# Turning softmax exponentials by VectorE blocks and DMAs instead of TensorE in a two-layer cross-attention kernel

## The chip, the cores and the metric

The kernel runs on one core of a Trainium2 chip, in float32. The metric is the device time of one execution in microseconds, as the median of several runs. The profile is one execution taken by the hardware profiler. Engines are named as the profile names them: PE is TensorE's matrix multiply and PEld its weight load, DVE is VectorE, ACT is ScalarE, POOL is GpSimd, SP is the engine that issues most DMAs. "L400" is line 400 of the kernel.

## The reference, cut to what matters

Two cross-attention layers follow one another over 8 batches of 256 rows with 320 channels; the context has 256 tokens of 512 channels. There are 20 heads of 16 channels in each layer.

```python
# layer 0: 77 text tokens and 179 image tokens, two separate softmaxes
q, k, v = heads(x @ Wq.T), heads(text @ Wk.T), heads(text @ Wv.T)
k_ip, v_ip = heads(ip @ Wk_ip.T), heads(ip @ Wv_ip.T)
a = softmax(q k^T / 4) v + softmax(q k_ip^T / 4) v_ip
x1 = merge(a) @ Wo.T + bo + x

# layer 1: 252 text tokens, 4 image tokens
q, k, v = heads(x1 @ W_q), heads(text @ W_k), heads(text @ W_v)
p = softmax(q k^T / 4);  text_out = p v
qsem = l2norm(p @ text);  sem = qsem @ l2norm(ip).T
p_ip = softmax(q k_ip^T / 4 + 0.5 * sem) * mask
out = merge(text_out + p_ip v_ip) @ W_out + b_out + x1
```

The norm of `qsem` is computed without forming it: with e the exponentials, the squared norm is the sum over tokens of (e G) * e, where G = text text^T.

## The kernel before, in words

**Tiling.** A unit of work is one batch and four heads (`QUADS`), so a batch has five units (NQ = 5) and each layer 40. For each head the scores of all 256 queries against 256 keys are put in one bank of PSUM (`sc`, two halves of 128 queries). VectorE takes the negative maxima (`l0_max`, L503; `l1_max`, L716), and ScalarE writes the exponentials to SBUF with queries on the partitions (`l0_exp`, L515; `l1_exp`, L731). The next product sums over the keys, so keys have to be on the partitions: `transposed_probs` (L400) has TensorE turn each head's exponentials in four 128-column pieces back into the head's own score bank, and one copy (L407) takes them to SBUF as `et`. That copy is VectorE's for three heads of four and ScalarE's for the other.

**The value products.** `l0_values` (L533) multiplies the values v0 with `et` for four heads at once. `l1_values` (L755, L758) takes, for each half of a head, `et` as weights and streams `gv`, which holds values, normalized image tokens and G side by side. VectorE then multiplies the G part by e and sums it (L762, a reduction with a read of its accumulator) and copies the 20 value columns (L766). The results `y` have two buffers in PSUM.

**The order of the work.** It is written out by hand. The loop over n from 0 to 45 runs layer 0's unit n and, from n = 6 on, layer 1's unit n - 6. `both_layers` (n < 40) writes out one period: layer 0's scores, maxima and exponentials, its transposes between the halves of the value products of the layer-1 unit before, then layer 1's scores, maxima, exponentials and transposes, and last `l0_values`. `layer_1` does n = 40 to 45. `fillers(n, place)` is a table that puts projections, output products and the other small work of four different batches into places 0 to 7 of a period. Each compute engine runs its instructions in the order in which they are written. `masked_q` (L352, POOL) makes the masked queries that the next scores take; `l1_image` has SP copy vipA into 80 rows by four DMAs (`vip_rows`, L662), and POOL masks them.

**Loads.** SP issues, in order: inputs of the batches ahead (`xT`, `encT`, `texts`, L128, L134, L437), the residual rows `x` (L141, POOL adds the bias), `vip_rows`, and the outputs (L896). `load_late` brings the weights that layer 1 and the output products take, `ip_sb` among them, after n = 0.

Of the kernel before, what the change touches and what calls it, by code (L numbers as in the profile page):

```python
# [43 lines left out]
W1 = WV + TC1  # L44
W2 = WV + TXT1
# [5 lines left out]
def kernel(  # L51
# [85 lines left out]
    def load_resid(b):  # L137

        r = bat[b]
        r["x"] = io.tile([P, NH, C], F32, tag="x", name=f"x_{b}", bufs=1)  # L140
        nc.sync.dma_start(out=r["x"], in_=x[b].rearrange("(n p) c -> p n c", p=P))  # L141
        for half in range(NH):
            nc.gpsimd.tensor_tensor(r["x"][:, half, :], r["x"][:, half, :], bo_b, ALU.add)
# [227 lines left out]
    def unit(layer, b, g, sc, home):  # L371

# [3 lines left out]

        def pairs(pool, shape, tag, bufs):
            return [
                pool.tile(list(shape), F32, tag=tag, name=f"{tag}_{name}_{x}", bufs=bufs)
                for x in range(2)  # L380
            ]

# [4 lines left out]
            "nmx": pairs(small, nmx, f"nmx{layer}", 4),  # L387
            "e": pairs(work, (P, 2, NH, T), f"e{home}", 2 + home),
            "et": pairs(work, (P, 2, 2, NH, P), f"et{home}", 2),
        }  # L390

    def transposed_probs(u, j, tn, t0, copy=None):


        x, i = divmod(j, 2)
        ps = u["sc"][j][:tn].rearrange("p n t -> p (n t)")
        v = ps.rearrange("p (c n s) -> p c n s", c=2, n=NH)
        for c in range(2):
            for half in range(NH):
                nc.tensor.transpose(  # L400
                    v[:, c, half, :],
                    u["e"][x][:, i, half, t0 + c * tn : t0 + (c + 1) * tn],
                    ident,
                )

        copy = copy or (nc.vector.tensor_copy if j < 3 else nc.scalar.copy)
        copy(u["et"][x][:tn, i].rearrange("p c n s -> p (c n s)"), ps)  # L407
# [8 lines left out]
    v0 = [const.tile([P, 2, H, 2, D], F32, tag=f"v0_{i}", name=f"v0_{i}") for i in range(2)]  # L416
    for t in v0:
        nc.gpsimd.memset(t[:, 1, :, 0, :], 0.0)
# [3 lines left out]
    W_K1 = T + TC1 + NIP  # L422
    k1 = const.tile([P, 2, W_K1], F32, tag="k1", name="k1")

    k1c = [const.tile([P, W_K1], F32, tag=f"k1c_{i}", name=f"k1c_{i}") for i in range(2)]

# [16 lines left out]
    def l0_k(b, m):  # L443
# [24 lines left out]
        else:  # L468
# [5 lines left out]
            for rows in (low, high):  # L474
                nc.scalar.copy(kc[rows, NIP + first : T], ps[high, t0 + first : t0 + TXT1])
                if kept:
                    nc.scalar.copy(kc[rows, NIP : NIP + TXT0], kt[high, m, :])
# [45 lines left out]
    def l0_transposed(u, j, copy=None):  # L523
        transposed_probs(u, j, P, 0, copy)
# [777 lines left out]
```

## Time and profile before

| what | value |
|---|---|
| median of 3 runs | 879.38 us (879.34 to 879.57) |
| span of the profiled execution | 877.6 us |
| what lies around the span | 1.8 us, median less span |
| TensorE matmul | 863.8 us busy, 98% |
| VectorE / ScalarE / GpSimd | 612.4 / 545.0 / 208.5 us busy |
| transposes of exponentials on TensorE (L400) | 1280, 182.4 us busy |
| their copies to SBUF (L407) | 229 on VectorE, 154.4 us; 91 on ScalarE, 52.2 us |
| granted TensorE clock | 1.000 |
| DMA | 22.96 MB in 24,624 packets |
| SBUF-to-SBUF DMAs | 32, of 25 KB each (`vip_rows`) |

A row of the profile's table of groups gives line, engine, operation, what is written and read, the shapes and the count; after the bar stand the busy time in us and the mean duration in ns of one; after the second bar the engine's idle time just before them, and what ended most of it. Durations of neighbours on one engine can overlap by some hundredths of a microsecond. In a timeline the two leading numbers are start and duration in us. A line of the chain in order of time names the work that nothing else hides. A row of a table by stretches has the stretch, its length, the busy time of PE, PEld, DVE, ACT and POOL with counts, the granted clock, the share of the 16 DMA engines and GB/s.

### The profile page before, as it was taken

The page shows a single profiled execution, that of the slowest core. Times are in us where ns is not written, and L with a number is a line of the kernel's source. Part 1 is how long each engine was busy: PE and PEld are TensorE (multiplying, and loading weights), DVE is VectorE, ACT ScalarE, POOL GpSimd, SP SyncE. Part 2 cuts the span into 40 slices and gives each one's busy share as a digit, 9 for nine tenths or more (in the row PEclk, how much of TensorE's full clock was granted, in tenths as well). Part 3 has the DMA queues.
Part 4 walks back from the last instruction along what each step waited for, and adds up shares of the span by engine and source line. Part 5 has one row for each costly group of instructions (what it writes and reads, how often), then busy time and mean ns, then how long its engine had stood idle before and what let it go on. Part 6 is the DMA issues. An engine that isn't in the chain of part 4 may idle for free.

```text
span 877.6 us, 18756 instructions
## 1 busy us (share of the span) xinstructions
PE 863.8 (98%) x6184; PEld 696.3 (79%) x6184; DVE 612.4 (70%) x2071; ACT 545.0 (62%) x2386; POOL 208.5 (24%) x376
## 2 busy tenths in 40 slices
PE   8999999999999999999999999999999999999998
PEld 6777678788787887888877888888888788777876
DVE  2544477767776777876778678776777778875765
ACT  4774676556664686555765468654675558754855
POOL 2212311223211222122321322212222122312111
PEclk9999999999999999999999999999999999999999
DMA  9600100001000100001001010000100100000000
GB/s 279 174 6 16 44 1 1 2 18 41 15 2 20 34 25 2 15 22 43 17 1 21 16 43 1 3 20 16 43 1 1 22 16 1 1 21 1 1 20 16
DMA packets 24624, 22.96 MB, mean 26 GB/s; under 512 B 5936, under 2 KB 24496, under 8 KB 24528
## 3 DMA queue, kind: packets, MB, share of 16 engines
q1 hardware_dynamic: 23088, 20.27, 8.8%
q10 hardware_dynamic: 1440, 1.49, 0.5%
q8 instruction: 50, 0.82, 0.4%
q14 instruction: 46, 0.38, 0.1%
HBM read 18.31 MB, written 2.62 MB: 24 GB/s over the span
## 4 chain that ended last, share of the span: by engine, by line
PE 95%; ACT 3%; DVE 1%; DMA 1%; issue 0%; SPq 0%; POOL 0%; ACTq 0%; DVEq 0%
PE y L755 17%; PE sc L400 16%; PE v L325 11%; PE sc L362 10%; PE y L758 9%; PE k L313 8%; PE q L295 7%; PE p_o L338 6%; PE oT L533 5%; PE g L624 2%; ACT e L515 1%; PE p_aT_ps L331 1%; ACT e L731 1%; PE o L553 1%; PE ipo L877 1%; DMA wk<-in_WkT_dram 1%
## 5 line engine op out<-in xcount | busy, mean ns | idle before, releaser
L515 ACT ACTIVATE e<-sc,nmx 128x77 f32<-128x77 f32 (+1 forms) x640 | 227.2, 412 | 57.4 <-DVE nmx L503 57.4
L731 ACT ACTIVATE e<-sc,nmx 128x252 f32<-128x252 f32 x320 | 147.4, 484 | 120.0 <-DVE aip L711 107.3
L755 PE MATMUL y<-gv,et 126*128 126x272 f32 x640 | 202.0, 397 | 1.3
L762 DVE CUSTOM_DVE_ANT_0 e<-y,e 128x252 f32<-128x252 f32 x320 | 133.9, 419 | 90.4 <-PE y L758 81.8
L400 PE MATMUL sc<-ident,e 128*126 128x128 f32 (+1 forms) x1280 | 182.4, 274 | 4.2 <-ACT e L731 2.8
L407 DVE COPY et<-sc 128x512 f32<-128x512 f32 (+1 forms) x229 | 154.4, 689 | 24.3 <-PE sc L400 14.5
L503 DVE TENSOR_REDUCE nmx<-sc 128x2 f32<-128x154 f32 x320 | 109.7, 416 | 87.2 <-PE sc L362 87.2
L400 PEld LDWEIGHTS sc<-ident,e 128*126 128x126 f32 (+1 forms) x1280 | 149.1, 140 | 14.2 <-ACT e L731 6.2
L515 ACT ACTIVATION_READ_ACCUMULATOR e<-sc,nmx 128x1 f32 x640 | 159.9, 250 | 0.0
L758 PEld LDWEIGHTS y<-gv,et 126*128 126x128 f32 x640 | 120.7, 189 | 25.9
L758 PE MATMUL y<-gv,et 126*128 126x146 f32 x640 | 131.4, 287 | 0.0
L716 DVE TENSOR_REDUCE nmx<-sc 128x2 f32<-128x504 f32 x160 | 106.7, 673 | 22.7 <-PE sc L362 22.7
L755 PEld LDWEIGHTS y<-gv,et 126*128 126x128 f32 x640 | 104.8, 190 | 18.2 <-issue 3.0
L568 POOL TENSOR_TENSOR attn<-o_sb 128x64 f32<-128x64 f32 x80 | 24.0, 321 | 396.3 <-DVE o_sb L558 355.2
L407 ACT COPY et<-sc 126x512 f32<-126x512 f32 (+1 forms) x91 | 52.2, 593 | 75.8 <-PE sc L400 75.7
L362 PE MATMUL sc<-k,sc_qz 32*128 32x256 f32 x1152 | 82.6, 400 | 1.0 <-ACT k L465 0.6
L352 POOL TENSOR_SCALAR sc_qz<-q,quad_m 128x256 f32<-128x256 f32 x80 | 73.2, 925 | 6.6 <-ACT q L302 6.0
L362 PEld LDWEIGHTS sc<-k,sc_qz 32*128 32x128 f32 x1152 | 52.1, 184 | 24.4 <-issue 15.3
L731 ACT ACTIVATION_READ_ACCUMULATOR e<-sc,nmx 128x1 f32 x320 | 69.7, 218 | 0.0
L325 PE MATMUL v<-wv,encT 128*126 128x324 f32 (+1 forms) x192 | 58.1, 447 | 0.0
L766 DVE COPY num<-y 128x20 f32<-128x20 f32 x320 | 55.6, 174 | 0.0
L338 PE MATMUL p_o<-wo,p_aT 128*128 128x320 f32 x180 | 53.0, 437 | 0.3 <-DVE p_aT L332 0.3
(148 smaller groups left out, 1044.7 us busy)
## 6 DMA issues: line engine op xcount, KB each, us to landing
encT<-in_encT_dram SPq DMA_DIRECT2D x7, 512.0 KB
x<-in_x_dram SPq DMA_DIRECT2D x8, 320.0 KB
out_dram<-osb SPq DMA_DIRECT2D x15, 160.0 KB
xT<-in_xT_dram SPq DMA_DIRECT2D x7, 256.0 KB
texts<-in_encT_dram SPq DMA_DIRECT2D x6, 154.0 KB
xT<-in_xT_dram SPq DMA_DIRECT2D x7, 128.0 KB
vip_rows<-vipA SPq DMA_DIRECT2D x32, 25.0 KB
wv<-in_WvT_dram SPq DMA_DIRECT2D x1, 640.0 KB
```

The lines of the kernel that those rows point to most:

```text
L325: nc.tensor.matmul(ps, lhsT(k), w[:, k, :], start=(k == 0), stop=(k == NE - 1))
L338: nc.tensor.matmul(ps[:, :C], aT[:, m, :], w[:, m, :], start=(m == 0), stop=(m == NC - 1))
L362: nc.tensor.matmul(sc[j][:, half, :], qz[rows, half * P : (half + 1) * P], kT(j)[rows, :], start=True, stop=True,)
L400: nc.tensor.transpose(v[:, c, half, :], u["e"][x][:, i, half, t0 + c * tn : t0 + (c + 1) * tn], ident,)
L407: copy(u["et"][x][:tn, i].rearrange("p c n s -> p (c n s)"), ps)
L503: nc.vector.tensor_reduce(u["nmx"][x][:, j, :, a], u["sc"][2 * x + j][:, :, t0:t1], AX.X, ALU.max, negate=True,)
L515: nc.scalar.activation(u["e"][x][:, j, half, t0:t1], u["sc"][2 * x + j][:, half, t0:t1], AF.Exp, bias=u["nmx"][x][:, j, half, a : a + 1], ...
L716: nc.vector.tensor_reduce(u["nmx"][x][:, j, :], u["sc"][2 * x + j][:, :, t0 : t0 + TXT1], AX.X, ALU.max, negate=True,)
L731: nc.scalar.activation(u["e"][x][:, j, half, t0 : t0 + TXT1], u["sc"][2 * x + j][:, half, t0 : t0 + TXT1], AF.Exp, bias=u["nmx"][x][:, j, ...
L755: nc.tensor.matmul(y, et[:, 1 - odd, half, :], gv[0][:, g, full], start=True, stop=False)
L758: nc.tensor.matmul(y[:, into], et[:, odd, half, :], gv[1][:, g, part], start=False, stop=True)
L762: nc.vector.tensor_tensor_reduce(e, y[:, g0 : g0 + TXT1], e, op0=ALU.mult, op1=ALU.add, scale=1.0, scalar=0.0, accum_out=r["n2"][:, half, ...
```

## The change

While both layers run, TensorE turns no exponentials. Instead:

- VectorE turns each head's exponentials in square blocks of 32 rows (`blocks`, two instructions a head of 256 elements per partition) into a tile `eb`. A block's rows then stand in the right order but on the wrong group of 32 partitions.
- `moved` has SP issue 16 DMAs for each unit of each layer. Each carries what lies on one group of 32 partitions and belongs on another (or the same) from `eb` to `et`: 64 KB, in pieces of 1 KB for layer 0 and 256 B for layer 1.
- The tiles e0 (layer 0's exponentials), eb0 and eb1 are taken in turn from one tag, "blk", of two buffers. Layer 1's exponentials get three fixed tiles `e1`, whose columns 252 to 255 are zero. Layer 0's `et` has one buffer, layer 1's two.
- `l0_values` of a unit moves to the next period, behind that period's layer-0 scores. Layer 1's value products stand behind the block transposes, two heads before layer 1's scores and two after.
- The layouts of keys and `gv` are simplified, so that odd and even heads share them; the first `y` product of an even head has 292 columns instead of 272. `v0c` holds the image-only part of layer 0's values once.
- The residual x is loaded into x1 directly, four periods later than before. `l0_v(1, 2)` and others shift places.
- `layer_1` keeps the transposes on TensorE; each head's copy becomes two on ScalarE.

```diff
+    def blocks(layer, u, j, src):
+        if "eb" not in u:
+            shape = (QB, 2, 4) if layer else (2, QB, 4)
+            u["eb"] = quad_tile("blk", f"eb{layer}_{u['b']}_{u['g']}", shape + INNER[layer], 2)
+        order = "p i x n -> p n i x" if layer else "p i n x -> p n i x"
+        for c in range(2):
+            nc.vector.transpose(
+                (u["eb"][:, :, c, j] if layer else u["eb"][:, c, :, j]).rearrange(order),
+                src[c].rearrange("p n (i x) -> p n i x", x=32),
+            )
+
+    def moved(layer, u):
+        turned(layer, u)
+        for i in range(QB):
+            for to in range(QB):
+                et = u["et"][32 * to : 32 * to + 32]
+                eb = u["eb"][32 * i : 32 * i + 32]
+                if layer:
+                    nc.sync.dma_start(
+                        out=et.rearrange("p c j i x n -> p (c j) i (x n)")[:, :, i],
+                        in_=eb[:, to].rearrange("p c j x n -> p (c j) (x n)"),
+                    )
+                else:
+                    nc.sync.dma_start(
+                        out=et[:, :, i].rearrange("p c j n x -> p c (j n x)"),
+                        in_=eb[:, :, to].rearrange("p c j n x -> p c (j n x)"),
+                    )
...
     def l0_begin(b, g):
...
+        u["e"] = quad_tile("blk", f"e0_{b}_{g}", (4, NH, T), 2)
...
     def both_layers(n, u, v1):
         u0 = l0_begin(*divmod(n, NQ))
+        part(l0_values, u)
         for pair in range(2):
             l0_max(u0, pair)
         l0_exp(u0, 0)
-        late = n > NQ and n % NQ == 3
-        if late:
-            l0_exp(u0, 1)
         fillers(n, 0)
-        if not late:
-            l0_exp(u0, 1)
-        part(l1_values, v1, 0, (0,))
-        l0_transposed(u0, 0)
-        part(l1_values, v1, 0, (1,))
-        l0_transposed(u0, 1)
+        l0_exp(u0, 1)
+        l0_blocks(u0, 0)
+        l0_blocks(u0, 1)
         part(l0_attn, u)
         fillers(n, 1)
-        part(l1_values, v1, 1, (0,))
-        l0_transposed(u0, 2)
-        part(l1_values, v1, 1, (1,))
-        l0_transposed(u0, 3, nc.vector.tensor_copy if n == 1 or n % NQ == 2 and n > 2 * NQ else None)
+        part(l1_values, v1, 0)
+        l0_blocks(u0, 2)
         fillers(n, 2)
-        part(l1_values, v1, 2)
+        part(l1_values, v1, 1)
+        l0_blocks(u0, 3)
+        moved(0, u0)
         qz[1] = queries(1, n)
         qz[0] = queries(0, n + 1)
         fillers(n, 3)
         u1 = begin1(n)
         for pair in range(2):
             part(l1_max, u1, pair)
         part(l1_exp, u1, 0)
         fillers(n, 4)
         part(l1_exp, u1, 1)
-        part(l1_values, v1, 3, (0,))
-        part(l1_transposed, u1, 0)
-        part(l1_transposed, u1, 1)
         fillers(n, 5)
-        part(l1_values, v1, 3, (1,))
-        part(l1_transposed, u1, 2)
-        part(l1_transposed, u1, 3)
+        for j in range(4):
+            part(l1_blocks, u1, j)
+            if j % 2:
+                part(l1_values, v1, 2 + j // 2)
+        part(lambda u: moved(1, u), u1)
         fillers(n, 6)
-        l0_values(u0)
         return u0, u1
...
-        if s == 1 and 0 < b < B:
-            load_resid(b)
+        if s == 0 and 1 < b <= B:
+            load_resid(b - 1)
```

## The prediction

> **What bounds the kernel now.** I read the page first: the share of each engine, then the chain of waits that ended last.
>
> ```profile
> PE 863.8 (98%) x6184; PEld 696.3 (79%) x6184; DVE 612.4 (70%) x2071; ACT 545.0 (62%) x2386; POOL 208.5 (24%) x376
> ...
> PE 95%; ACT 3%; DVE 1%; DMA 1%; issue 0%; SPq 0%; POOL 0%; ACTq 0%; DVEq 0%
> PE y L755 17%; PE sc L400 16%; PE v L325 11%; PE sc L362 10%; PE y L758 9%; PE k L313 8%; PE q L295 7%; PE p_o L338 6%; PE oT L533 5%; PE g L624 2%; ACT e L515 1%; PE p_aT_ps L331 1%; ACT e L731 1%; PE o L553 1%; PE ipo L877 1%; DMA wk<-in_WkT_dram 1%
> ```
>
> TensorE is the bound: 95% of the chain, 16% of it turning exponentials (L400). Next, the chain in order of time, 398 to 420 us, prices one head (start, us, what):
>
> ```profile
> 402.25 0.46 PE y L755 x2
> 402.71 0.25 PE y L758 x2
> 402.96 0.44 PE sc L400 x4
> ...
> 413.46 0.89 PE sc L400 x8
> ```
>
> A head's four transposes cost 0.44 us of chain; a half of a layer-1 value product costs 0.46 + 0.25 = 0.71 us. Layer 0's scores start at 89.88 us (n = 6) and at 768.04 us (n = 39): 33 periods of 20.55 us in which both layers run.
>
> **What goes.** The changed program's order shows that it does what it says: 1,184 of 1,280 transposes leave TensorE, 96 stay behind the both-layer phase. 296 heads x 0.44 = 130 us, 3.5 us of a period. TensorE needs then about 17.1 us of 20.55, and 747 us in all is a floor. With them go the copies L407: 4.2 us of VectorE per period (141.93 us from 89.90 to 790.30) and 1.1 us of ScalarE (36.37 us).
>
> **What comes, per period.** Sixteen VectorE block transposes of 256 elements per partition, and 32 DMAs from SP, each 32 partitions x 2 KB = 64 KB, 16 for each layer. The trace holds no such transpose. Nearest rows by operation and shape:
>
> ```profile
> L558 DVE TENSOR_TENSOR o_sb<-o,rden 128x256 f32<-128x256 f32 x40 | 16.6, 415 | 2.7 <-PE o L553 2.7
> ...
> L174 DVE MEMSET zeros<- 128x256 f32 x1 | 0.3, 272 | 0.9 <-PEq L1284 0.9
> ```
>
> It is at least the 0.27 us fill (as many elements written to SBUF), at most 0.69 us (L407, 512 elements, two passes). I take 0.33 us from one start to the next, since it is SBUF to SBUF and starts on VectorE overlap ends by some 0.07 us. The Trainium skill (VectorE: DVE Perf Modes, section "The three transpose paths") gives 311 ns for 128x128 bf16; with 128 more elements an estimate is 0.44 us, and by it the forecast would be some 30 us higher.
>
> The price that matters is SP's. Its timeline (start, us):
>
> ```profile
> 406.09 0.39 SPq L128 DMA_DIRECT2D xT<-in_xT_dram  x1
> 406.53 0.46 SPq L129 DMA_DIRECT2D xT<-in_xT_dram  x1
> ...
> 428.92 1.88 SPq L437 DMA_DIRECT2D texts<-in_encT_dram  x2
> ...
> 784.29 1.52 SPq L662 DMA_DIRECT2D vip_rows<-vipA  x2
> ```
>
> A lone issue takes 0.37 to 0.39 us, the one behind it 0.46 us; the next can start about 0.04 us later. The first transfers of the run start 0.48 to 0.64 us apart. The only SBUF-to-SBUF rows, vip_rows, take 0.75 us each, but read one partition and write 20. I take s = 0.50 us (full partitions, back to back), and keep 0.37 and 0.75 as ends. Sixteen issues are then 8.0 us. The transfer itself hides behind the issue: the residual load moves at 314 GB/s
>
> ```profile
> 86.80:87.20 0.40, 0.40 (x3) 0.35 (x3) 0.00 (x0) 0.00 (x0) 0.00 (x0) 1.00 0.86 314
> ```
>
> (last column), or 0.21 us for 64 KB. Layer 1's pieces are 256 B, so its share may be worse, and is not priced apart. From the end of the last issue to the consumer: that load was issued by 85.28, its packets start about 0.6 us later, and POOL starts 0.4 us after its last; with 0.3 to 0.5 us of packets I take 1.5 us (ends: 0.9, and the 2.3 us from vip_rows' last issue, 850.95, to POOL at 853.23).
>
> Here a rule of the skill stands against my reading. DMA: Bandwidth & Descriptors, section "Issuing engines are not separate DMA queues", holds that a sequencer's issue time is usually small beside the DMA. In these rows it is the larger, 0.37 to 0.75 us against 0.21 us. By the rule 16 DMAs would cost some 3.4 us, a period 17.4 us, and the kernel some 790 us.
>
> **Where the waits fall.** The tag "blk" has two buffers and three users a period: e0, eb0, eb1. So layer 0's turned blocks of n+1 are written where eb1 of n lies. The first block transpose of n+1 waits on VectorE until layer 1's 16 DMAs of n have landed (call this L), and its whole queue stands behind it: value reductions, layer 1's maxima, layer 1's blocks. TensorE waits at the first y product for the same DMAs; ScalarE's first exponential waits for layer 0's. This makes a ring, in us after L:
>
> - VectorE's pitches, from its timeline 398 to 421 us: 0.49 for a value reduction with its two small operations (403.00 to 403.49), 0.35 for o_sb. From first to last layer-0 block: 8 x 0.33 + 0.35 + 4 x 0.49 = 5.0, with 0.5 for fillers and TensorE's second y: 5.5.
> - Layer 0's DMAs issue from 5.5 to 13.5.
> - Beside them layer 1's scores, maxima (four in 2.7 us, 410.87 to 413.53), exponentials (eight in 4.2 us, 411.72 to 415.9) and blocks: 5.5 + 0.5 + 2.7 + 8 x 0.33 + 2 x 0.49 = 12.3, so SP is later by about a microsecond.
> - Layer 1's DMAs issue from 13.5 to 21.5 and land at 23.0, the next L.
>
> A period is max(5.5 + 16s, 12.5) + 16s + 1.5 = **23.0 us**, against 20.55. TensorE at 17.1, VectorE at 15.5 - 4.2 + 16 x 0.33 = 16.6 and ScalarE at 13.2 - 1.1 = 12.1 all fit (15.5 and 13.2 from their busy time of 77.73 and 65.86 us in the batch 294.02 to 398.64). So do the wider y products (292 columns for 272 in even heads, 0.07 us a head) and the strided operands: even if the value products' weight loads (0.19 us, 1,280 for 160 heads) took twice as long and none of it overlapped, they would add 6.1 us a period, TensorE's whole slack of 5.9 us. Where that slack is gone, the wider products cost 0.3 us a period.
>
> **The rest.** (a) SP's order puts layer 0's first 16 DMAs ahead of three rows of ip_sb and all later weights, behind 1.8 MB of loads issued by 14.7 us. TensorE reaches the first layer-0 values waiting, some 7 us late; later layer-0-only periods are 3.1 + 8.0 + 1.5 = 12.6 us against 11 to 14. I add 7 us. (b) In the first period of a batch the residual load comes behind layer 1's 16 DMAs and the four vip_rows issues (3 us) behind it; POOL waits for both ahead of the masked queries. I add 1.5 us x 7 = 10. Where POOL is not caught, nothing. (c) The tail gets two ScalarE copies for one, some 0.23 us x 24 heads, and one late landing: 5 us. Layer 0's values, moved past the next scores, and out's two issues a batch (0.36 us each) are within these.
>
> Sum against the profiled execution: 877.6 + 33 x 2.45 + 7 + 10 + 5 = 980.5 us of span. The median of the runs, 879.38, lies 1.8 above the span: **982 us**. I call 0.2% (1.8 us) what a measurement can tell from no change.
>
> **Rivals.**
> - *The hand-over is cheap* (faster): if issues overlap to s = 0.37 and landing is 0.9, SP no longer closes the ring: max(5.0 + 5.9, 11.8) + 5.9 + 0.9 = 18.6 us, with 9 us for start and tail 877.6 - 33 x 1.95 + 9 + 1.8 = 824 us. With that landing it decides below about s = 0.40. For: lone issues at 0.37. Against: every second issue at 0.46. 13%.
> - *SBUF-to-SBUF issues cost 0.75*, as vip_rows: 5.5 + 12 + 12 + 1.5 = 31 us, 33 x 10.45 + 22 + 879.4 = 1,246 us. For: the same kind of path. Against: every 128-partition row. 13%.
> - *The block transpose takes two passes*, 0.65 us a start: blocks end at 8.1, layer 1's at 17.4, period 17.4 + 8.0 + 1.5 = 26.9 us, 1,111 us. For: nothing shows its rate. Against: every VectorE row here runs near one element per ns. 9%.
>
> **How the numbers follow.** The ring with s near 0.5 has 65%: s = 0.41 gives a period of 20.6 and some 902 us, s = 0.60 gives 26.2 and 1,088 us. The range, 860 to 1,150 us, holds these, the two-pass case and the edges of the others. Faster than 0.2%: the first rival, 0.13. Same: 0.02, from the low edge of the forecast. Slower: 0.85.
>
> **What would show it.** Right: the chain carries SP's issue and DMA waits instead of 95% TensorE; VectorE's longest wait is the block transpose on the layer-1 transfer; SP's issues stand shoulder to shoulder at about 0.5 us; layer 0's scores come about 23 us apart; TensorE falls to some 75%. Wrong: TensorE above 90%, or transposes at 0.6 us with SP idle. The weakest term is s: each 0.05 us is 1.6 us a period, 53 us in all.

## The result and the profile after

The changed kernel takes 1,304.04 us (median of four runs, 1,302.82 to 1,312.78); the kernel before, run beside it, 879.45 us (879.34 to 879.57). The ratio is 1.485, 95% interval 1.481 to 1.489. The forecast was 982 us, 860 to 1,150: the sign was right, the loss four times as large as put down (424.6 us for 102.6), and the time lies outside the range. The profiled execution has a span of 1,301.1 us.

From the page of the changed kernel: TensorE's line of the engine table, and the two lines of the chain that ended last, by engine and by line of code.

```profile
PE 911.8 (70%) x5000; PEld 668.7 (51%) x5000; DVE 652.2 (50%) x2434; ACT 505.1 (39%) x2319; POOL 196.5 (15%) x354
...
PE 34%; SPq 34%; DVE 16%; DMA 7%; issue 5%; ACT 3%; POOL 0%; DVEq 0%; ACTq 0%; POOLq 0%
SPq L418 24%; PE y L793 13%; SPq L423 9%; DVE blk_eb L405 6%; DMA et<-blk_eb 6%; PE y L794 5%; DVE nmx L546 4%; PE k L315 3%; PE sc L364 3%; PE p_o L340 3%; ACT e L763 2%; DVE e L798 2%; PE v L327 2%; DVE nmx L749 2%; PE q L297 1%
```

The instructions of TensorE fell from 6,184 to 5,000 as planned, yet its busy time rose, at a mean granted clock of 0.828 in place of 1.000, and the chain, 95% TensorE before, is now a relay in which SP's issue (SPq) has as large a part as TensorE. L423 issues layer 0's moves and L418 layer 1's; oT (L576) is the product of `l0_values`. Some of the waits (us in all, times, longest):

```profile
DVE blk_eb L405 <- DMA et<-blk_eb: 352.4, 32, 13.5
ACT e L763 <- DVE aip L745: 309.0, 34, 15.3
ACT oT_sb L586 <- PE oT L576: 303.5, 40, 16.7
...
PE y L793 <- DMA et<-blk_eb: 146.7, 31, 6.7
```

No engine is short of time; each waits for another. VectorE's longest wait is the one that the prediction named, the block transpose on a move's landing, once in each of some 32 periods. One period in order of time (start, us, engine, line; xN is how many instructions the piece holds; the last line is cut off where the window ends):

```profile
601.29 10.33 SPq L423 DMA_DIRECT2D et<-blk_eb  x16
...
611.00 1.42 DVE L405 STREAM_TRANSPOSE blk_eb<-e 128x256 f32<-128x256 f32 x4
...
612.45 10.76 SPq L418 DMA_DIRECT2D et<-blk_eb  x16
...
625.07 1.42 DVE L405 STREAM_TRANSPOSE blk_eb<-blk_e 128x256 f32<-128x256 f32 x4 [6.18 <-DMA et<-blk_eb]
...
626.86 1.34 PE L793 MATMUL y<-gv,et 126*128 126x292 f32 x2 [0.77 <-DVE o_sb L601]
...
631.26 0.76 DVE L405 STREAM_TRANSPOSE blk_eb<-blk_e 128x256 f32<-128x256 f32 x2
632.04 1.25 SPq L423 DMA_DIRECT2D et<-blk_eb  x2
```

That is the whole ring. Layer 0's move is issued from 601.29 to 611.62, layer 1's from 612.45 to 623.21. Between them SP stands free for 0.8 us, until layer 1's last block ends at 612.42; that is so in 6 of 33 periods. In the other 27 layer 1's blocks are done 0.8 to 4.6 us before its move starts, and the move waits behind layer 0's on SP's queue. Layer 1's move lands at 625.07, where VectorE's blocks, 6.18 us late, and TensorE's products start; the last layer-0 block ends at 632.02, and at 632.04 the next move begins. From one move of layer 0 to the next: 30.75 us. TensorE, VectorE and ScalarE all have holes in it.

To say where the 423.5 us of span went, I read from VectorE's timeline when the first maxima of layer 0 start for unit 6 and unit 39. Between them lie 33 periods.

| kernel | unit 6 (us) | period (us) | from unit 39 to the end (us) | span (us) |
|---|---|---|---|---|
| before | 91.0 | 20.55 | 108.4 | 877.6 |
| after | 153.0 | 30.69 | 135.3 | 1,301.1 |
| difference | 62 | 33 x 10.14 = 335 | 27 | 423.5 |

### The profile page after: what moved, and what is told of

Read it like the earlier page. It is cut to its first block, busy times and chain, and to the rows that moved or that the text cites. A ratio compares the mean times of both kernels' runs of the same rounds, so it can differ in the third digit from the quotient of the medians.

```text
span 1301.1 us, 18067 instructions
## 1 busy us (share of the span) xinstructions
PE 911.8 (70%) x5000; PEld 668.7 (51%) x5000; DVE 652.2 (50%) x2434; ACT 505.1 (39%) x2319; POOL 196.5 (15%) x354
## 4 chain that ended last, share of the span: by engine, by line
PE 34%; SPq 34%; DVE 16%; DMA 7%; issue 5%; ACT 3%; POOL 0%; DVEq 0%; ACTq 0%; POOLq 0%
SPq L418 24%; PE y L793 13%; SPq L423 9%; DVE blk_eb L405 6%; DMA et<-blk_eb 6%; PE y L794 5%; DVE nmx L546 4%; PE k L315 3%; PE sc L364 3%; PE p_o L340 3%; ACT e L763 2%; DVE e L798 2%; PE v L327 2%; DVE nmx L749 2%; PE q L297 1%
## 5 line engine op out<-in xcount | busy, mean ns | idle before, releaser
L793 PE MATMUL y<-gv,et 126*128 126x292 f32 (+1 forms) x640 | 267.7, 506 | 191.7 <-DMA et<-blk_eb 146.7
L405 DVE STREAM_TRANSPOSE blk_eb<-blk_e 128x256 f32<-128x256 f32 x320 | 118.7, 417 | 451.6 <-DMA et<-blk_eb 352.4
L793 PEld LDWEIGHTS y<-gv,et 126*128 126x128 f32 x640 | 125.4, 236 | 225.8 <-issue 196.2
L558 ACT ACTIVATE blk_e<-sc,nmx 128x77 f32<-128x77 f32 (+1 forms) x640 | 226.7, 401 | 2.4 <-DVE nmx L546 2.1
L794 PEld LDWEIGHTS y<-gv,et 126*128 126x128 f32 x640 | 150.8, 236 | 44.3 <-issue 5.1
L798 DVE CUSTOM_DVE_ANT_0 e<-y,e 128x252 f32<-128x252 f32 x296 | 121.2, 410 | 98.5 <-PE y L794 94.5
L576 PE MATMUL oT<-et,v 128*32 128x256 f32 x320 | 37.5, 552 | 169.4 <-DMA et<-blk_eb 138.7
L794 PE MATMUL y<-gv,et 126*128 126x146 f32 x640 | 155.9, 331 | 0.0
L558 ACT ACTIVATION_READ_ACCUMULATOR blk_e<-sc,nmx 128x1 f32 x640 | 153.2, 240 | 0.0
L586 ACT COPY oT_sb<-oT 128x256 f32<-128x256 f32 x40 | 14.9, 373 | 303.5 <-PE oT L576 303.5
L546 DVE TENSOR_REDUCE nmx<-sc 128x2 f32<-128x154 f32 x320 | 108.9, 412 | 30.0 <-PE sc L364 29.7
L576 PEld LDWEIGHTS oT<-et,v 128*32 128x32 f32 x320 | 8.4, 129 | 184.4 <-issue 159.9
L405 DVE STREAM_TRANSPOSE blk_eb<-e 128x256 f32<-128x256 f32 x272 | 95.9, 410 | 0.1
L763 ACT ACTIVATION_READ_ACCUMULATOR e<-sc,nmx 128x1 f32 x296 | 64.4, 218 | 0.0
L327 PEld LDWEIGHTS v<-wv,encT 128*126 128x126 f32 (+1 forms) x192 | 46.5, 255 | 34.5 <-issue 27.7
```

The source lines that it names most:

```text
L327: nc.tensor.matmul(ps, lhsT(k), w[:, k, :], start=(k == 0), stop=(k == NE - 1))
L405: nc.vector.transpose((u["eb"][:, :, c, j] if layer else u["eb"][:, c, :, j]).rearrange(order), src[c].rearrange("p n (i x) -> p n i x", x ...
L546: nc.vector.tensor_reduce(u["nmx"][x][:, j, :, a], u["sc"][2 * x + j][:, :, t0:t1], AX.X, ALU.max, negate=True,)
L558: nc.scalar.activation(u["e"][:, 2 * x + j, half, t0:t1], u["sc"][2 * x + j][:, half, t0:t1], AF.Exp, bias=u["nmx"][x][:, j, half, a : a + 1],
L763: nc.scalar.activation(u["e"][x][:, j, half, :TXT1], u["sc"][2 * x + j][:, half, :TXT1], AF.Exp, bias=u["nmx"][x][:, j, half : half + 1], ...
L793: nc.tensor.matmul(y[:, :n], et[1], gv[0][:, g, first:W2], start=True, stop=False)
```

## The experiments

The theory after the result: a move lasts as long as its issues on one queue, sixteen at 0.645 us from start to start, and two moves of one period stand in a ring with VectorE and TensorE. The rivals: the bytes or landings set the length of a move (transfers); the waits on moves are bystanders; TensorE's clock, which falls while it waits, is the loss. The times below are single runs beside a run of the kernel before (878.9 to 879.6 us); the columns are those of the table above. The changed kernel's four runs spread over 10 us, and the run with rows of idle DMAs, the same program up to its end, has unit 6 at 157.9 us and a period of 30.85. Differences of that size are not read.

| run | time (us) | unit 6 | period | end part |
|---|---|---|---|---|
| three buffers | 1,301.4 | 155.4 | 30.21 | 147.2 |
| three buffers, blocks first | 1,213.3 | 152.2 | 27.71 | 145.0 |
| two queues (ScalarE) | 1,164.9 | 134.5 | 27.45 | 122.8 |
| four issues | 978.1 | 130.6 | 22.04 | 118.4 |
| eight more issues | 1,468.1 | 156.5 | 35.27 | 146.0 |
| blocks first, GpSimd's queue | 1,157.4 | 133.7 | 26.78 | 138.1 |
| the same, queries first | 1,085.4 | 133.6 | 24.71 | 134.3 |
| three buffers, 12 + 4 issues, scores first | 1,166.8 | 118.8 | 27.50 | 138.8 |
| layer 0 alone | 932.0 | 122.0 | 20.94 | 117.3 |
| layer 0 alone, GpSimd's queue | 928.7 | 118.5 | 21.20 | 108.9 |
| idle products | 1,352.6 | 155.8 | 31.89 | 142.8 |
| late copy of oT | 1,316.4 | 172.8 | 30.50 | 135.5 |
| start with oT late | 1,282.9 | 128.4 | 30.83 | 135.3 |
| rows of idle DMAs at the end | 1,404.8 | 157.9 | 30.85 | 227.0 |

### What an issue costs (f1_forms)

```diff
+    for a, b_, i, t in pairs:                       # sixteen: 32 partitions, one piece of 2 KB
+        nc.sync.dma_start(out=dst[b_, i], in_=src[a, t])
+    for i in range(4):                              # four: 128 partitions by 2 KB
+        nc.sync.dma_start(out=dst[:, i], in_=src[:, i])
...
```

> The changed kernel with rows of idle DMAs after its end, each kind by itself, to read the issue time of each from the records (they move zeros between two spare buffers and touch no output): on SP, sixteen of 32 partitions by 2 KB in one piece to another partition group; four of 128 partitions by 2 KB; sixteen of 32 partitions by eight pieces of 256 B; sixteen of 32 partitions by 512 B; sixteen from DRAM of 32 partitions by 1 KB; sixteen of one partition by 2 KB; then eight of the first kind on GpSimd's queue and eight on ScalarE's. Theory (an issue has a fixed price): all on SP at 0.45 to 0.65 us, whatever their bytes and pieces. Rival A (price by descriptors): one partition below 0.2 us, 128 partitions above 1.5 us, pieces of 256 B above those of 2 KB by half or more. Rival B (price by source): from DRAM 0.37 to 0.47, between buffers on the chip 0.58 to 0.61. The whole takes 40 to 90 us longer than 1,304.

1,404.8 us, 101 more than 1,304 where 40 to 90 were expected: the rows stand one behind the other, each kind waiting for the landing of the one before. The issue rows (count: shortest/median/longest ns, first and last start), in the order of the text, without the kind of 512 B and ScalarE's:

```profile
L1277 SPq DMA_DIRECT2D blk_form_dst<-blk_form_src x16: 577/588/596, 1312.9 to 1322.4; - x16
...
L1280 SPq DMA_DIRECT2D blk_form_dst<-blk_form_src x4: 476/540/601, 1327.1 to 1329.1; - x4
...
L1283 SPq DMA_DIRECT2D blk_form_dst<-blk_form_src x16: 608/610/693, 1333.9 to 1343.8; - x16
...
L1292 SPq DMA_DIRECT2D blk_form_dst<-in_encT_dram x16: 332/419/421, 1361.9 to 1369.0; - x16
...
L1296 SPq DMA_DIRECT2D blk_form_dst<-blk_form_src x16: 538/587/591, 1373.1 to 1382.5; - x16
L1299 POOL DMA_DIRECT2D blk_form_dst<-blk_form_src x8: 496/497/703, 1387.2 to 1390.8; - x8
```

Between SBUF tiles a row of one partition costs as much as one of 32, and 64 KB as much as 256 KB: 0.54 to 0.61 us. The price is fixed and rival A falls. Rival B holds for DRAM: from there an issue into SBUF takes 0.42 us. But this run changed only the source, and the source is not the whole of it. In the kernel before, the outputs go from SBUF to DRAM, and the image rows from SBUF to SBUF:

```profile
L896 SPq DMA_DIRECT2D out_dram<-osb x14: 338/357/410, 264.3 to 849.1; - x14
...
L662 SPq DMA_DIRECT2D vip_rows<-vipA x32: 707/730/851, 58.6 to 850.2; - x32
```

So the dear rows are those with both ends in SBUF, and of these the kernel before had only `vip_rows`. That is the part that the prediction missed. From start to start it is 0.63 us on SP ((1322.4 - 1312.9) / 15), 0.51 on GpSimd's queue and 0.64 on ScalarE's, whose eight rows have a median of 0.55.

The timeline of the first two kinds also parts issues from bytes. Both carry 1 MB in pieces of 2 KB, and VectorE's next fill waits for the landing:

```profile
1312.94 10.09 SPq L1277 DMA_DIRECT2D blk_form_dst<-blk_form_src  x16
1325.34 1.76 DVE L1278 MEMSET blk_form_dst<- 128x2048 f32 x1 [12.54 <-DMA blk_form_dst<-blk_form_src]
1327.13 2.47 SPq L1280 DMA_DIRECT2D blk_form_dst<-blk_form_src  x4
1332.07 1.76 DVE L1281 MEMSET blk_form_dst<- 128x2048 f32 x1 [4.97 <-DMA blk_form_dst<-blk_form_src]
```

From the first issue to that fill it is 12.4 us in sixteen issues and 4.9 us in four.

### Issues against bytes (g3_eight_more, e4_four_issues, e3_two_queues)

```diff
     def moved(layer, u):
+        if layer:
+            for i in range(8):
+                nc.sync.dma_start(out=spare[:, i], in_=u["eb"][:1, i // 4, 0, i % 4, 0])
```

> The changed kernel with eight idle DMAs of 8 bytes on SP's queue ahead of each layer-1 move, into a spare tile: next to no bytes, eight more issues. Theory (the period is a ring in which every issue of the layer-1 move counts with its full price of 0.60 to 0.645 us): 34 periods longer by 4.8 to 5.2 us, 1,465 to 1,485 us in all. Rival (the moves are bound by their bytes or their landing, and the queue has room): less than 2 us a period, below 1,375 us.

1,468.1 us, in the theory's range. The eight (0.553 us each) stand ahead of the layer-1 move from 609.33 to 614.41, 5.08 us, and the period is 4.58 us longer for 64 bytes, a little less than the 4.8 to 5.2 expected.

```diff
-            for to in range(QB):                    # sixteen of 32 partitions by 2 KB
+            nc.sync.dma_start(out=u["et"][32*i : 32*i+32], in_=u["eb"][32*i : 32*i+32])  # four by 8 KB
```

> The same bytes move, but in four DMAs of 32 partitions by 8 KB a unit instead of sixteen of 32 partitions by 2 KB; left out is the carrying between partition groups (a block goes to the partitions that it is already on), so the probabilities are not transposed across groups. Theory (an issue costs about 0.6 us whatever it moves up to here): a move takes 4 x 0.6 = 2.6 us of issue and then some 2 to 4 us until the last lands; period 17 to 22 us, 870 to 1,020 us in all. Rival A (the time goes by bytes or descriptors): an issue takes 2.4 us, the move 10 us, 1,304 us within 30. Rival B (transfers are the limit): issues are short but the wait for the landing grows by what they save, 1,250 us or more.

978.1 us: the same bytes in a quarter of the issues take away 8.65 us of the period, 85% of the steady loss. (The pieces are larger too, 8 KB instead of 256 B and 1 KB; that issues count at equal pieces, and without bytes, is shown by the two kinds of 2 KB pieces above and by the eight idle issues.) The period, 22.04, is at the theory's upper edge, because the transfers now show. In the chain of this kernel, after the last issues of a layer-1 move:

```profile
591.76 0.66 SPq L415
592.46 5.21 DMA et<-blk_eb
```

From the start of the last issue the landing takes 5.2 us here, and 2.5 us in the period of the changed kernel shown above (0.6 of issue and 1.9), where issuing is slower than carrying. This whole move, four issues from 590.58 and the landing at 597.67, takes 7.1 us where the changed kernel's takes 12.6 (612.45 to 625.07). The other 14.9 us of its period are what layer 1 needs from a landing to its last block (14.9 on average in this kernel, 15.6 in the changed one). So issues are the limit, and behind them wait some 7 us of carrying and the chain of layer 1.

```diff
+                eng = nc.sync if i % 2 == 0 else nc.scalar
-                    nc.sync.dma_start(
+                    eng.dma_start(
```

> Half of the sixteen issues of each move go to ScalarE's queue, the rest stay on SP's; bytes, pieces, order and buffers stay as in the changed kernel. Theory (a move lasts as long as its issues on one queue): each of the two moves takes about 8 x 0.65 = 5.2 us plus 1.9 of landing in place of 10.5 plus 1.9, the ring falls by up to 10.5 us to 20 to 22, but ScalarE's waiting issues now stand ahead of its exponentials; period 21 to 26 us, 1,000 to 1,160 us in all. Rival (the 1 MB of transfers sets the length of a move): moves stay at 10 to 11 us, 1,304 us within 20.

1,164.9 us: a large gain, which excludes the rival, and 5 us outside the theory's range. A move's issues now take 5.5 us (layer 0) and 6.8 us (layer 1) in the mean, but the period falls by 3.2 us only, to 27.45, above the 21 to 26 expected. ScalarE's exponentials wait behind its own issues:

```profile
587.82 3.87 ACTq L424 DMA_DIRECT2D et<-blk_eb  x6
591.79 0.47 ACT L764 ACTIVATE e<-sc,nmx 128x252 f32<-128x252 f32 x1 [4.52 <-DMA et<-blk_eb]
```

### Where the ring closes (e1, e2, c1, g2, b1)

```diff
-quad_tile("blk", ..., 2)        # et1: 2 buffers
+quad_tile("blk", ..., 3)        # et1: 1 buffer
```

> Three buffers instead of two for the tiles of exponentials and blocks (blk); et1 has one buffer instead of two to make room, and the order of the program stays. Theory (a ring of two moves on SP's queue, 7.0 + 10.4 + 0.7 + 10.8 + 1.9 = 30.7 us a period): the third buffer frees block transposes from the layer-1 transfer, but VectorE's blocks 2 and 3 of layer 0 still stand behind the reductions of the first layer-1 products, which need that same transfer, so one loop stays closed; period 28 to 30.5 us, 1,215 to 1,300 us in all. Rival A (the second buffer of blk is the whole cause): period about 22, 1,020 us. Rival B (the block transposes' wait is a bystander): 1,304 us within 10.

1,301.4 us, period 30.21: the buffer alone is not the cause, rival A falls. The time cannot tell the theory (up to 1,300) from rival B (1,304 within 10); the trace can. The block transposes' wait for the move fell from 352.4 to 28.5 us, but VectorE's wait for the products y, which need the same transfer, rose from 94.5 to 283.9. So that wait by itself is a bystander, as in rival B, because a second one stands beside it, as in the theory.

```diff
+        l0_blocks(u0, 2)
+        l0_blocks(u0, 3)
+        moved(0, u0)
         fillers(n, 1)
         part(l1_values, v1, 0)
```

> As the kernel with three buffers, and all four layer-0 block transposes and the layer-0 move stand ahead of the fillers and of the first layer-1 products in program order. Theory (ring): both waits on the layer-1 transfer are now off the way to the next move, and what is left is SP's own queue, 16 x 0.645 + 16 x 0.67 = 21.1 us of issue a period; period 21.5 to 24 us, 1,010 to 1,080 us in all, SP's issues shoulder to shoulder. Rival A (the loop closes elsewhere, through ScalarE's or TensorE's order): period 27 to 30, 1,190 to 1,290 us. Rival B (transfers, not issues, set the length of a move): moves grow when they follow each other without a gap, period 26 or more.

1,213.3 us, period 27.71: rival A. Its period also lies in rival B's interval, but the moves did not grow (10.5 and 10.8 us of issue, 10.3 and 10.7 in the changed kernel). The layer-0 move left the ring, but SP's queue did not become the bound. From its timeline:

```profile
578.94 1.26 PE L793 MATMUL y<-gv,et 126*128 126x292 f32 x2 [4.65 <-DMA et<-blk_eb]
...
583.77 1.15 PE L364 MATMUL sc<-k,sc_qz 32*128 32x256 f32 x16
...
591.89 0.59 SPq L418 DMA_DIRECT2D et<-blk_eb  x1
```

A second loop runs through layer 1 alone: its move lands at 578.94; TensorE's program has the first products y ahead of the next layer-1 scores, which start at 583.77; maxima, exponentials and blocks follow, and the next layer-1 move starts at 591.89. That is 12.95 us, with 11.3 of issue and 1.7 to land 26 us; on average over 33 periods it is 15.2, 10.8 and 1.9 us.

```diff
+                eng = nc.sync if i % 2 == 0 else nc.gpsimd      # on top of the edit before
```

> Three buffers and layer-0 blocks first, as in the run that gave 1,213 us, and eight of the sixteen issues of each move on GpSimd's queue. Theory (after the blocks are put first, the loop is landing, first products y, layer-1 scores, exponentials and blocks 12.9 us, then the layer-1 move 11.3, then 1.7 until it lands): the layer-1 move falls to 5.2 us, the loop to 19.8, a period of 19.5 to 21.5 us, a start some 25 us shorter; 900 to 980 us in all. Rival A (GpSimd's queue, which makes the masked queries and spreads the gram rows, is held up by waiting issues): period 23 to 26, 1,030 to 1,130 us. Rival B (transfers of two queues slow each other): moves of 8 us or more, period 23 or more.

1,157.4 us, period 26.78, above rival A's 23 to 26, by its mechanism. GpSimd's instruction that makes the masked queries stands behind its waiting issues, and the scores behind that (85.0 us in 29 waits of TensorE):

```profile
569.76 4.25 POOL L424 DMA_DIRECT2D et<-blk_eb  x8 [2.96 <-DVE nrm L834]
574.01 1.15 POOL L677 COPY gv<-gv 126x1134 f32<-126x1134 f32 x1
575.13 1.83 POOL L354 TENSOR_SCALAR sc_qz<-q,quad_m 128x256 f32<-128x256 f32 x2
577.17 0.74 PEld L364 LDWEIGHTS sc<-k,sc_qz 32*128 32x128 f32 x16
```

Rival B holds as well: from its first issue to the first product that reads it a layer-1 move takes 9.5 us in the mean, not 6.9.

```diff
+        qz[1] = queries(1, n)
+        qz[0] = queries(0, n + 1)
         moved(0, u0)
```

> As the run with three buffers, blocks first and half of the issues on GpSimd (26.8 us a period), but the masked queries of the next scores are made by GpSimd ahead of its share of the layer-0 move. Theory (there the layer-1 scores waited for queries that stood behind GpSimd's waiting issues; without that the loop is 12.9 + 5.2 + 1.7 us): period 20 to 23 us, 920 to 1,020 us in all. Rival A (GpSimd's issues hold up something else, the gram rows or fused products): period 24 to 27, 1,060 to 1,160 us. Rival B (a move on two queues is no shorter for its reader than on one): no change, 1,157 us within 10.

1,085.4 us, period 24.71, in rival A's range, but what else GpSimd's issues might hold up was not found; that wait for the queries is down to 3.1 us in all. The queries were worth 2.1 us a period. The rest of the miss is in two parts, in the mean of 33 periods: a move on two queues takes 9.5 us to its first reader instead of 6.9, and from there to the next layer-1 move it is 15.5 instead of 12.9. The chain, one layer-1 move:

```profile
569.32 0.59 SPq L419
...
572.86 1.15 SPq L419
...
575.23 2.99 DMA et<-blk_eb
```

SP's last issues take 1.1 us, and the move lasts 8.9 us from 569.32 to 578.22; the way from there to the next layer-1 move was 17.5 us in this period (578.22 to 595.68), with the projections of the output and the attention's transposes in it.

One more version took the three buffers, twelve of sixteen issues on SP and four on ScalarE, and put the layer-1 scores ahead of the first products:

```diff
+        u1 = begin1(n)                  # scores of layer 1
+        part(l1_exp, u1, 0)
         part(l1_values, v1, 0)
```

> Both layers by blocks, with three buffers for blk and one for et1, twelve of the sixteen issues of a move on SP's queue and four on ScalarE's, the layer-0 move and the layer-1 scores ahead of the first layer-1 products, and oT after the fillers. Theory (the loop left in the kernel with blocks first runs landing, y products, exponentials, layer-1 move): a move now takes 12 x 0.65 = 7.8 us, the loop about 7 + 7.8 + 1.9 = 16.7 us, and TensorE bounds the period at 17.1 to 19.5 us; 800 to 890 us in all. Rival A (waiting issues hold up ScalarE's exponentials, 12.1 + 8 x 0.65 = 17.3 us of work and stalls): period 22 to 25, 950 to 1,060 us. Rival B (the transfers of two moves get in each other's way): moves of 10 us and more, period 24 or more.

1,166.8 us, period 27.5: the time is a miss for every case. The moves take 9.2 (layer 0) and 8.6 us (layer 1) to issue, not 7.8, and the place where this order loses the rest was not isolated. In this kernel the last unit of a batch uses image values and rows of the next batch; no instruction is left out for it.

### One layer alone (a1, a2)

```diff
+        for j in range(4):              # layer 0: blocks and one move
+            l0_blocks(u0, j)
+        moved(0, u0)
+        part(l1_transposed, u1, 0, nc.vector.tensor_copy)   # layer 1: on TensorE, as before
```

> One part alone: only layer 0's exponentials are turned in blocks and moved (sixteen issues a unit); layer 1 is turned by TensorE and copied as in the kernel before, with no layer-1 move; the product oT stands after the fillers instead of at the head of the period. Theory (two moves closing a ring through SP's queue and VectorE are the whole loss): the one move of 10.5 + 1.9 us hides in a period that TensorE bounds at 20.55 - 4 x 0.44 = 18.8 us; about 34 x 1.76 = 60 us less than the kernel before, 815 to 860 us in all, below 879. Rival A (any move on the way costs its whole length): period 22 to 24, 930 to 1,000 us. Rival B (the block transposes and strided operands themselves cost): period 20 to 21, 875 to 900 us.

(In this kernel the last unit of a batch is multiplied with the next batch's image values.) 932.0 us, period 20.94. One move hides: TensorE waits 0.12 us a period for it (3.7 us in thirty). That two moves in a ring make the loss holds, the expected gain does not: 1.76 us a period were to come back and none did. The time lies in rival A's interval and the period in rival B's, but A's mechanism is not there and B's is only a part. TensorE's groups over thirty periods of this kernel (180.59 to 808 us), columns busy, mean ns, idle before:

```profile
L789 PE MATMUL y<-gv,et 126*128 126x292 f32 (+1 forms) x478 | 161.7, 419 | 15.9 <-DVE o_sb L597 10.3 <-DVE num L799 4.3
L364 PE MATMUL sc<-k,sc_qz 32*128 32x256 f32 x864 | 80.0, 406 | 0.1
```

and over thirty of the kernel before (110.44 to 726.94 us):

```profile
L755 PE MATMUL y<-gv,et 126*128 126x272 f32 x478 | 149.8, 394 | 0.5
...
L362 PE MATMUL sc<-k,sc_qz 32*128 32x256 f32 x848 | 60.8, 400 | 0.0
```

The wider products cost (161.7 - 149.8) / 30 = 0.4 us a period; the scores 0.0926 - 0.0717 us each, or 0.6 (that they wait inside their rows for the banks that the last copy empties is a reading, not shown); oT, in two groups of 19.2 and 18.7 us for 240 each against 31.0 for 464, another 0.2; and TensorE's idle time went from 0.9 to 23.0 us, 0.7 a period, most of it for VectorE's readings of y and o, which the transposes used to cover. That is 1.9 of the 2.1 us that are missing (1.76 saved, and a period 0.36 longer all the same). Where TensorE is 98% busy by such a tight weave, what is taken out leaves holes.

> Layer 0 alone by blocks, as in the kernel with one part alone, but with eight of a move's sixteen issues on GpSimd's queue, and from the sixth period on the product oT at the end of its own period, as in the kernel before; while layer 0 runs alone it stands behind the fillers of the next period. Theory (the 20.9 us of the one-part kernel's period come from where oT stands, which leaves TensorE's scores waiting for the last copy of layer 1 and the products y close behind each other, and from wider products): the move takes 8 x 0.62 + 1.9 = 6.9 us and lands before oT is due; period 19.3 to 20.2 us, start within 15 us of the kernel before; 850 to 890 us in all. Rival A (the move cannot be hidden): TensorE waits for the landing at oT, period 21 to 23, 900 to 960. Rival B (GpSimd's issues delay the masked queries that the scores need): the same time, with scores waiting for GpSimd.

Eight issues of the move on GpSimd's queue, and oT back at the end of its own period: 928.7 us, period 21.20. The steady part did not gain. Time and period lie in rival A's ranges, but none of the three cases has the place right. TensorE waits 4 us in all for the landing between 160 and 800 us, none for the queries, and 21.5 us for VectorE between products y. Of the span that the two kernels with one part lose (52.7 and 49.4 us), 31 and 27.5 lie ahead of unit 6, where layer 0 runs alone, and only 13 and 21 in the 33 steady periods.

### The clock (e5) and the start (e6, g1)

```diff
+            for i in range(16):
+                nc.tensor.matmul(ps[:, :S], ident, k0[:, 0, :], start=True, stop=True)
         part(l1_values, v1, 0)
```

> Sixteen idle products of the identity with 256 columns, into a spare PSUM tile, stand ahead of the first layer-1 products of each period, so that TensorE does not stand still while it waits for the layer-1 transfer; they use nothing that is late. Theory (TensorE's clock falls in that wait, and the first products then take 1.2 to 1.3 us where 0.62 to 0.74 is usual, on the way to the blocks and the next move): 1 to 1.5 us less a period, 1,250 to 1,275 us in all. Rival A (the clock falls for other reasons, or the slow products are not on the way): 1,304 us within 8. Rival B (the idle products are themselves in the way): 1,310 to 1,400 us.

1,352.6 us: rival B. The sixteen run as 32 passes, and in about every fifth period their PSUM tile is late:

```profile
573.54 10.22 PE L1197 MATMUL warm<-k,ident 128*128 128x256 f32 x32 [7.80 <-DVE attn L923]
583.59 0.66 PE L793 MATMUL y<-gv,et 126*128 126x292 f32 x2
```

The products behind them do take 0.66 us and not 1.2 to 1.3. The granted clock (last column but two) shows it: behind a wait of 4.61 us in the changed kernel it is 0.50, and behind idle products that end after the landing it is 1.00:

```profile
533.00:537.00 4.00, 3.96 (x10) 2.99 (x11) 2.67 (x12) 0.00 (x0) 2.35 (x4) 0.50 0.00 0
...
543.00:547.00 4.00, 4.00 (x24) 3.33 (x25) 3.40 (x16) 0.00 (x0) 2.40 (x4) 1.00 0.00 0
```

These two are the same period. In the run with idle products its layer-1 move lands at 542.53 us and the next move starts 5.7 us later, at 548.25; in the changed kernel it is 6.95 us (532.84 to 539.79), and the products between take 1.25, 1.27, 1.11 and 0.66 us in place of 0.62 to 0.70. So the slow products are on the way and cost 1.2 us in this period. Over the 28 periods from unit 6 on without that stall the length stays the same on average (single ones -1.3 to +1.3 us): elsewhere the gain and the price of the idle products cannot be told apart. The mean granted clock of the run rose from 0.828 to 0.896 and the time did not fall, so no more than about 1.2 us a period is shown to be the clock's.

```diff
-        nc.scalar.copy(u["o"], o)          # ahead of the sixteen exponentials
+        part(l0_copied, u)                 # behind them
```

> The copy of oT out of PSUM stands behind a unit's sixteen exponentials in ScalarE's program order instead of ahead of them; nothing else. Theory (while layer 0 runs alone, that copy makes the exponentials wait for the landing of the move before, so that landing, exponentials, blocks and move follow each other): the five such periods fall from 23 to 32 us to 14 to 20 us, the steady periods stay at 30.7 within 0.3; 1,255 to 1,280 us in all. Rival A (the start is slow because the move waits behind the weight loads on SP): the start keeps its length within 5 us, 1,300 us. Rival B (the later copy delays the transposes of oT in the steady part): period 31 or more.

1,316.4 us, unit 6 at 172.8 instead of 153.0: the theory of this run fell. The exponentials are free of the copy, but the transposes of oT on TensorE, with projections behind them, now wait for it:

```profile
68.70 0.42 ACT L589 COPY oT_sb<-oT 128x256 f32<-128x256 f32 x1
...
69.17 0.44 PE L599 MATMUL o<-ident,oT_sb 128*128 128x128 f32 x2 [3.68 <-ACT oT_sb L589]
```

So the product itself was moved, behind fillers, exponentials and blocks, while layer 0 runs alone:

```diff
+        if not first:
             part(l0_values, u)
...
+            fillers(n, 1)
+            part(l0_values, u)
```

> The changed kernel, but while layer 0 runs alone (except the sixth period) the product oT and its copy stand behind the fillers, the exponentials and the blocks of the next unit; the periods in which both layers run are unchanged. Theory (at the start, oT at the head of TensorE's and ScalarE's queues holds the projections and exponentials until the move has landed): the scores of the seventh unit start at 115 to 130 us in place of 151.8, the steady period stays at 30.7; 1,268 to 1,285 us in all. Rival (the start is slow because a move of 12.4 us follows each unit's blocks, wherever oT stands): 151.8 within 8 us, 1,296 to 1,310 us.

1,282.9 us, unit 6 at 128.4, the period unchanged. Some 25 of the 62 us of the start come from where oT stands. Two queues without that edit bring unit 6 to 134.5, 18.5 us less, so the length of the move has a part too; the two were not tried together.

## Why the prediction was wrong

- **The ring was right.** The chain, VectorE's longest wait, the two moves in a row and 33 longer periods came as written; they are 335 of the 423.5 us. Its links, as means of 33 periods read from SP's and VectorE's timelines: from a landing to layer 0's move 7.6 us (put down: 5.5), issuing that move 10.25 (8.0), from the landing to layer 1's last block 15.6 (12.3), issuing layer 1's move 10.7 (8.0), landing 1.8 (1.5). The prediction's own formula gives with them max(7.6 + 10.25, 15.6) + 10.7 + 1.8 = 30.4 us; 30.69 was measured. In six of these periods layer 1's blocks come last (up to 19.9), and in six others loads stand between the two moves on SP's queue.
- **The step that failed is s.** "I take s = 0.50 us (full partitions, back to back)". Measured from start to start: 0.645 for layer 0, 0.67 for layer 1.

```profile
L423 SPq DMA_DIRECT2D et<-blk_eb x640: 585/595/1136, 21.0 to 1197.8; - x160
```

The row is 0.595 us, and 0.05 lies between rows. The two moves take 4.9 us more than put down, of 7.7 us by which the period was missed: with s = 0.50 the measured links give max(7.6 + 8.0, 15.6) + 8.0 + 1.8 = 25.4 us. Of the 321 us of span by which the forecast was missed, s is then some 162 (33 x 4.9), the other links 92, less the 10 of (b), the start 55 and the end 22. The value came from rows with one end in DRAM. The row that was set aside, vip_rows with 0.75 us, was the only one with both ends in SBUF, and that was what counted; its single partition did not (0.587 for one). Why vip_rows costs 0.73 and not 0.59 stays open. The ends 0.37 and 0.75 held the value, and the rival with 0.75 (a period of 31 us, 1,246 us in all) came nearest, with too high a price and too small other terms.
- **The other terms of the ring.** Landing to layer 0's move is 2.1 us longer: the products between the blocks took 1.1 to 1.3 us instead of 0.7, on a TensorE that had stood still, which the idle products show to be worth 1.2 us in the period that could be read. The prediction had no term for the clock. Layer 1's chain is 3.4 us longer; in the period shown above its scores start at 603.53, behind an output projection of 3.4 us, but that such fillers are the whole cause was not tested.
- **The start: 62 us for 7.** The prediction priced a period of layer 0 alone as a move and its neighbours, 12.6 us. It did not ask what stands behind oT in the queues of TensorE and ScalarE once it is moved to the head of the period. The periods were 23 to 32 us.

```profile
79.67 1.08 PE L576 MATMUL oT<-et,v 128*32 128x256 f32 x8 [11.81 <-DMA et<-blk_eb]
```

TensorE waits 11.81 us here, then come the copy at 81.72 and the exponentials from 81.99: landing, copy, exponentials, blocks and move in a row.
- **The end: 27 us for 5**, read from the table only; its end part is 118.4 with four issues in place of 135.3, but what makes it was tested by no run. Term (b), 10 us for the first periods of a batch, is told apart by no run either.
- **Right.** A block transpose, from start to start 0.34 us (four in 1.42) for 0.33; its row is 0.41 to 0.42 us. The Trainium skill's figure (VectorE: DVE Perf Modes, section "The three transpose paths") led to an estimate of 0.44 us for the row, which is near. The strided operands cost oT 0.2 us a period, where the one-layer kernel lets it be read, and were covered in the ring.
- **The rule weighed against it.** By the Trainium skill (DMA: Bandwidth & Descriptors, section "Issuing engines are not separate DMA queues") issuing is usually small beside the transfer. For 64 KB between SBUF tiles this case shows the reverse: 0.645 us from issue to issue against 0.31 to 0.44 (1 MB in the 4.9 us of the four idle rows and in the 7.1 us of the move with four issues, divided by sixteen). The prediction was right not to follow it, and that the transfers hide behind the issues was right too.

No version tried comes below the kernel before. The nearest, one layer by blocks, is 928.7 us.

## What to carry to other kernels

Price a DMA issue by a row with the same two ends, and count issues before bytes: between SBUF tiles a 64 KB piece costs its queue as much as 256 KB. When a stage becomes a hand-over, write down every loop that it closes, for each queue whose order the program fixes: a third buffer, a second queue and a reordering each opened one here and met the next. A product moved ahead of others on an in-order engine is charged with all that stands behind it, above all where nothing else is there to run, as at the start.

## What the runs showed of the hardware

- An issue with both ends in SBUF takes 0.54 to 0.61 us on SP for 1 to 128 partitions, one to eight pieces each and 512 B to 2 KB per partition; 8 bytes take 0.553 (but vip_rows, from one partition to 20, 0.73). From DRAM into SBUF it is 0.42 for 32 partitions by 1 KB, from SBUF to DRAM 0.34 to 0.41. GpSimd's queue starts one between SBUF tiles every 0.51 us.
- A load from DRAM directly behind a move costs more as well: the residual rows' issue has a median of 0.60 us in the changed kernel, 0.40 in the one before.
- A layer-1 move (256 B pieces) whose issues are shared by SP and GpSimd has SP's rows stretched from 0.60 up to 1.15 us in the period shown, and takes 9.5 us from its first issue to its first reader; all of it on one queue 12.5.
- After 4 to 4.6 us without work TensorE's granted clock was 0.50 and its first products took 1.11 to 1.34 us, where 0.62 to 0.74 is usual; behind idle products it was 1.00, and they took 0.62 to 0.70.
